# An instruction-ordering model that knows shared SBUF ports, one-piece filter loads and a new table of priorities

## The chip, the cores and the metric

The kernel runs on one core of one Trainium2 chip. The metric is the device time of one execution in microseconds; the profile has, beside it, the span from the first to the last instruction. TensorE (PE) multiplies matrices, VectorE (DVE), ScalarE (ACT) and GpSimd (POOL) work element by element, and SyncE (SP) issues all DMAs here. The engines run beside each other and wait for each other by semaphores; each runs its own instructions strictly in the order in which the program lists them.

## The reference

Two layers, each an attention and a feed-forward part, with a residual and a layer norm after each part. The input is (2, 1024, 128) in float32.

```
x = LN(x + L0_attn(x))   # 8 heads, 16 wide keys, softmax over 1024; heads summed after a reshape
x = LN(x + L0_ffn(x))    # silu(x@w1)*(x@w2), two 512x512 layers with gelu, back to 128
x = LN(x + L1_attn(x))   # 4 heads: causal convolutions, a delta rule in chunks of 32
                         # (inverse of a 32x32 triangular matrix per chunk, then a scan over chunks),
                         # a short filter (3 taps) and a long one (31 taps) on the values, gates
x = LN(x + L1_ffn(x))    # weights of +-1: 256 -> 512 -> 512 -> 128 with relu
```

## The kernel before

The rows are cut into four groups of 512, called 00, 01, 10 and 11 (batch and half). Attention of layer 0 goes in eight units (two per group): `pass1` computes the scores for the row maxima (matmuls at L814, maxima by VectorE at L816), `pass2` computes them again transposed, takes the exponential on ScalarE (L856) and multiplies with the values (L861, four 32-column matmuls at a time). `ffn0` is the feed-forward part of layer 0 (matmuls at L894, each in split precision with a high part `ahi` and a low part `alo`), `l1_attn` the delta-rule attention, and `ffn1` the last part (L1370, L1371). A group's four parts follow each other; in layer 1 a half also needs the half before it of the same batch (state of the scan, edges of convolutions and filters).

Inside `l1_attn` the stages have labels: `l1prep` and `l1gate` (projections; convolutions at L1049), `l1gram`, `l1inv` (15 steps of a product at L1144 and a sum at L1145 on VectorE, then transposes at L1155), `l1v`, `l1fir` (short filter on the vector engines, long filter as 128 small matmuls, L1210, with matrices `toep` loaded in eight pieces of 128 KB by SP, L1206, into two buffers that take turns, `nm` and `pr`), `l1T` and `l1wu` (groups of four 32x32 matmuls, one per head, L996), `l1scan` (16 dependent steps: a matmul and an addition on VectorE, L1322), `l1out`, and `l1rms` (L1354 to L1362). Layer norms take statistics on VectorE (L699, L701), the root on GpSimd (L703, L704) and the normalisation on one of them (L706).

The program is first written down part after part, and then the whole of it is put in order by a planner. `Plan.graph` builds the dependences, `Op.price` gives every instruction a duration, `Plan.run` plays the program through in time: whenever an engine is free it takes, of the instructions whose inputs are there, the one with the best rank. The rank is the time to the end along the longest chain (after `TURNS` passes back and forth), less a bonus for the part and group that the instruction belongs to, from the table `AHEAD` (in thousands of nanoseconds). The order in which the model took the instructions becomes the order on each engine, by dependences that need no waiting (`order`).

Four more numbers are in `RUN`. `switch` is what TensorE must gain in rank before it changes between full 128x128 matmuls and tiled small ones. `target` is the sum of columns that it should have streamed in the last 3.4 us of the model's time; below it, a dense matmul is taken first, and where nothing is ready, a filler matmul on the identity is put in (`dummies`; L1516 for a full one, L996 with the tile `ip` for a group of four small ones). With `rewarm` off this stops while the model holds the clock to be low.

In the model VectorE and GpSimd are independent of each other: an instruction takes its price, whatever the other engine does.

Of the kernel before, what the change touches and what calls it, by code (L numbers as in the profile page):

```python
# [14 lines left out]
AX = mybir.AxisListType  # L15

MARK = HOOK = None
RUN = {'dummies': True, 'target': 4530, 'rewarm': False, 'switch': 7026}
TURNS = 5
AHEAD = {  # L20
    "ffn0": {"00": 22.2, "01": 18.7, "10": 2.9, "11": -654.8},
    "ffn1": {"00": -153.5, "01": -136.6, "10": -65.1, "11": 9.8},
    "l1T": {"00": 30.9, "01": -81.4, "10": 95.8, "11": -6.2},
    "l1fir": {"00": -18.8, "01": -105.5, "10": -8.4, "11": 28.7},
    "l1gate": {"00": 182.7, "01": -69.9, "10": 117.6, "11": 47.2},
    "l1gram": {"00": -32.0, "01": -18.3, "10": 34.2, "11": 45.9},
    "l1inv": {"00": 41.3, "01": -12.8, "10": 61.1, "11": -56.0},
    "l1out": {"00": -63.2, "01": 33.9, "10": -9.7, "11": -10.5},
    "l1prep": {"00": 20.1, "01": 18.8, "10": 57.7, "11": 43.0},
    "l1rms": {"00": 20.0, "01": 21.9, "10": 36.6, "11": -17.4},  # L30
    "l1scan": {"00": 19.3, "01": 27.2, "10": 70.9, "11": 82.5},
    "l1v": {"00": -69.1, "01": 37.5, "10": 176.4, "11": 55.1},
    "l1wu": {"00": -18.4, "01": 13.4, "10": 15.7, "11": -37.6},
    "norm_in": {"0": 108.6, "1": -14.8},
    "pass1": {"0": 5.1, "1": -21.2, "2": -75.6, "3": -562.6, "4": 17.7, "5": 65.3, "6": 18.4, "7": 4.4},
    "pass2": {"0": -83.4, "1": -75.7, "2": -184.7, "3": 31.0, "4": 13.6, "5": 203.8, "6": 15.6, "7": 28.5},
    "post": {"00": -35.5, "01": 102.2, "10": 132.9, "11": 164.2},
    "prep": {"": 106.5},
    "stacks": {"00": 29.8, "01": 8.9, "10": 191.8, "11": -5.2},
    "stk": {"0": 105.8, "1": 140.3, "2": -27.7, "3": 95.0, "4": -83.8, "5": 45.2, "6": 57.1, "7": 134.2},  # L40
    "weights": {"": 217.5},
}
HALVES, RU = 1, 1
LEND = (4, 2)
# [35 lines left out]
class Op:  # L80


    def __init__(self, ins, n):
        self.ins, self.n = ins, n
        self.preds, self.succ = {}, []
        self.table = None
        self.cols = self.occ = self.dur = self.data = self.load = 0
        self.mode, self.dense, self.parts = None, False, [ins]
        self.e = "-"
        if ins is None:  # L90
            return
        self.e = str(ins.engine).split(".")[1]
        ap = lambda a: getattr(a, "bass_ap", None)
        self.src = [ap(a) for a in ins.ins if ap(a) is not None]
        self.dst = [ap(a) for a in ins.outs if ap(a) is not None]
        self.price()

    def price(self):
        i, kind = self.ins, type(self.ins).__name__
# [12 lines left out]
        e = self.e  # L112
# [25 lines left out]
        if e == "Activation":  # L138
            t = (51 if psum(self.src[0]) else 93) + N / 1.2 + 93 * ptr
            f = str(getattr(i, "func", "")).split(".")[-1]  # L140
            self.table = {"Gelu": 1, "Exp": 0}.get(f)
        elif e == "DVE":
            t = {"InstBNStats": 69, "InstReciprocal": 150}.get(kind, 68) + N / (0.57 if kind == "InstStreamTranspose" else 0.96) + 61 * ptr
            sb = not any(map(psum, self.src + self.dst))
            if sb and kind in ("InstTensorScalarPtr", "InstTensorCopy", "InstMemset") and sum(size(a) > 1 for a in self.src) < 2:
                t -= N / 1.92
        else:
            op = str(getattr(i, "op", ""))
            if kind == "InstMemset":
                t = 36 + N / 1.2  # L150
            elif kind == "InstTensorCopy":
                t = 120 + (0.9 if N > 200 else 3.33) * N
            elif kind == "InstTensorTensor":
                t = 150 + (180 * N if "pow" in op else 2.1 * N)
            else:
                t = 765 if ptr == 2 and N == 128 else 175 + 0.97 * N + 75 * ptr
# [3 lines left out]
class Plan:  # L160
# [205 lines left out]
    def run(self, rank, switch=0, dummies=False, target=0, rewarm=False, least=-1):  # L366
# [6 lines left out]
        ready = {e: {} for e in list(LAT) + ["-"]}  # L373
        pend, times = [], [0.0]
        free, cnt, order = dict.fromkeys(ready, 0.0), {}, {e: [] for e in ready}
        table, idle, gone_at, queue = 0, 0, None, 0
        mode, end = None, 0.0
        recent, busy = [], 0
        todo = sum(o.e == "PE" for o in ops)

        def count(t, o, cols):
# [15 lines left out]
        while len(done) < len(ops):  # L397
# [4 lines left out]
            for e, qs in ready.items():  # L402
                while free[e] <= t:
# [24 lines left out]
                                continue  # L428
                    if not best:
                        break  # L430
                    o = heapq.heappop(qs[min(best)[2]])[2]
                    occ, dur, nxt = o.occ, o.dur, t + o.occ
                    if e == "PE":
                        todo -= 1
# [30 lines left out]
def body(ctx: ExitStack, tc: tile.TileContext, A, out, dbg=None):  # L465
# [536 lines left out]
    def l1_attn(L, gi, late):  # L1002
# [178 lines left out]
        def fir():  # L1181
# [21 lines left out]
            for d in range(32):  # L1203
                if d % 4 == 0:
                    toep = own(("nm", "pr")[d // 4 % 2], (128, 2, 4, 32))
                    nc.sync.dma_start(out=toep, in_=A["toep"][:, :, d:d + 4, :].rearrange("g p d c -> p g d c"))  # L1206
                for h in range(4):
                    g, e = divmod(h, 2)
                    s = slice(64 * e, 64 * e + 64)
# [318 lines left out]
def layout(inputs):  # L1528
# [66 lines left out]
    for t in range(32):  # L1595
        w = pad[:, 31 - t:95 - t].reshape(2, 2, 32, 2, 32)
        for j in range(2):
            tp[:, :, 1 - j, t] = w[:, :, :, j]
    d["toep"] = tp.reshape(2, 128, 32, 32)
    k0 = f["L1_ffn_k0"].view(np.uint8).reshape(2, 128, 512)  # L1600
    k1 = f["L1_ffn_k1"].view(np.uint8).reshape(4, 128, 4, 128).transpose(2, 1, 0, 3).reshape(4, 128, 512)
    k2 = f["L1_ffn_k2"].view(np.uint8).reshape(4, 128, 128).transpose(1, 0, 2).reshape(1, 128, 512)
# [16 lines left out]
```

## Time and profile before

| | |
|---|---|
| runs shown | 639.54 us median of 3 (631.74, 639.54, 640.3) |
| profiled execution | 634.86 us, span 633.1 us |
| mean granted TensorE clock | 0.956 |
| instructions | 18276 |
| busy: PE, weight loads, DVE, ACT, POOL | 564.3, 366.4, 435.2, 335.0, 254.6 us |
| chain that ended last | PE 47%, DVE 14%, issue 4%, ACT 4%, DMA 2%, POOL 2% |

How to read it: shares over the whole span hide that the kernel has stages. Up to some 380 us attention and `ffn0` of the first groups run together, and afterwards `l1_attn` and `ffn1` of all four groups are left, with many small dependent instructions. A view of the trace by stretches gives busy time and granted clock for each. "issue" in the chain is time in which an engine waited for nothing that the profile shows. The matmuls' ends are modelled, so a busy PE is not one at its peak.

### The profile page before, as it was taken

The page shows a single profiled execution, that of the slowest core. Times are in us where ns is not written, and L with a number is a line of the kernel's source. Part 1 is how long each engine was busy: PE and PEld are TensorE (multiplying, and loading weights), DVE is VectorE, ACT ScalarE, POOL GpSimd, SP SyncE. Part 2 cuts the span into 40 slices and gives each one's busy share as a digit, 9 for nine tenths or more (in the row PEclk, how much of TensorE's full clock was granted, in tenths as well). Part 3 has the DMA queues.
Part 4 walks back from the last instruction along what each step waited for, and adds up shares of the span by engine and source line. Part 5 has one row for each costly group of instructions (what it writes and reads, how often), then busy time and mean ns, then how long its engine had stood idle before and what let it go on. Part 6 is the DMA issues. An engine that isn't in the chain of part 4 may idle for free.

```text
span 633.1 us, 18276 instructions
## 1 busy us (share of the span) xinstructions
PE 564.3 (89%) x7767; PEld 366.4 (58%) x7767; DVE 435.2 (69%) x1002; ACT 335.0 (53%) x599; POOL 254.6 (40%) x347
## 2 busy tenths in 40 slices
PE   2879999999999999999999998789878987689984
PEld 1245355567565565465545675566656675567773
DVE  5869777774748956748694279953879787256773
ACT  3676467755858657958778662422644220024331
POOL 9783020230403323404445972364716547124310
PEclk9999999999999999999999999989999598578998
DMA  8786220225122233131023330544202112201220
GB/s 281 256 278 235 51 50 2 47 83 145 59 68 81 37 113 104 34 107 63 1 67 103 118 119 18 183 120 149 73 5 85 37 54 71 64 27 64 77 97 17
DMA packets 30691, 57.63 MB, mean 91 GB/s; under 512 B 4049, under 2 KB 16977, under 8 KB 30610
## 3 DMA queue, kind: packets, MB, share of 16 engines
q1 hardware_dynamic: 30610, 56.47, 29.1%
q8 instruction: 61, 1.00, 0.6%
q14 instruction: 20, 0.16, 0.1%
HBM read 40.40 MB, written 8.39 MB: 77 GB/s over the span
## 4 chain that ended last, share of the span: by engine, by line
PE 47%; DVE 14%; issue 4%; ACT 4%; DMA 2%; POOL 2%; POOLq 0%; SPq 0%; DVEq 0%; ACTq 0%
PE ps L894 12%; PE ps L996 6%; PE s L854 5%; PE pv L861 5%; PE ps L814 3%; PE ps L1370 3%; PE ps L1371 3%; PE ps L1210 2%; DMA nm<-toep 2%; DVE cv L1049 2%; DVE nm L1145 1%; DVE pr L1144 1%; PE ps L1036 1%; PE ps L712 1%; DVE mp L816 1%
## 5 line engine op out<-in xcount | busy, mean ns | idle before, releaser
L816 DVE TENSOR_REDUCE mp<-ps 128x1 f32<-128x512 f32 x224 | 141.1, 683 | 56.9 <-PE ps L814 56.5
L856 ACT ACTIVATE p<-s 128x512 f32<-128x512 f32 x236 | 130.9, 601 | 42.6 <-PE s L854 34.5
L894 PE MATMUL ps<-ahi,w 128*128 128x512 f32 x352 | 119.9, 411 | 1.6 <-DVE u L926 0.9
L814 PE MATMUL ps<-k,q 128*128 128x512 f32 x240 | 87.7, 423 | 4.2 <-DVE m L822 1.6
L854 PE MATMUL s<-q,k 128*128 128x512 f32 x236 | 89.7, 420 | 0.2
L894 PEld LDWEIGHTS ps<-ahi,w 128*128 128x128 f32 x352 | 63.7, 189 | 23.5 <-issue 2.7
L861 PE MATMUL pv<-p,va 128*32 128x512 f32 x512 | 73.3, 603 | 0.0
L894 PE MATMUL ps<-alo,w 128*128 128x512 f32 x176 | 71.0, 406 | 1.9 <-POOL alo L909 1.8
L814 PEld LDWEIGHTS ps<-k,q 128*128 128x128 f32 x240 | 43.9, 188 | 35.8 <-DVE mp L816 16.4
L854 PEld LDWEIGHTS s<-q,k 128*128 128x128 f32 x236 | 42.2, 188 | 32.5 <-ACT p L856 19.6
L1370 PE MATMUL ps<-ahi,w 128*128 128x512 f32 x96 | 41.6, 434 | 2.5 <-DVE alo L1386 2.5
L931 POOL TENSOR_TENSOR alo<-u,ahi 128x512 fp32r<-128x512 f32 x16 | 20.6, 1284 | 54.2 <-ACT ahi L930 54.2
L1371 PE MATMUL ps<-alo,w 128*128 128x512 f32 x96 | 41.4, 431 | 0.1
L894 PEld LDWEIGHTS ps<-alo,w 128*128 128x128 f32 x176 | 33.3, 189 | 12.1 <-POOL alo L909 3.5
L1385 ACT ACTIVATE ahi<-ps 128x512 fp32r<-128x512 f32 x32 | 18.7, 597 | 36.3 <-PE ps L1371 36.1
L1049 DVE SCALAR_TENSOR_TENSOR cv<-pj,cvh,cv 128x512 f32<-128x512 f32 x36 | 30.5, 848 | 8.7 <-ACT cv L1045 8.2
L789 POOL MEMSET q<- 2x1024 f32 x5 | 4.7, 948 | 65.7 <-PE s L854 37.0
L703 POOL TENSOR_SCALAR r<-mv 128x4 f32<-128x4 f32 (+1 forms) x24 | 5.6, 236 | 58.7 <-DVE mv L701 58.1
L1386 DVE SCALAR_TENSOR_TENSOR alo<-ps,ahi 128x512 fp32r<-128x512 f32 x32 | 21.6, 685 | 10.9 <-ACT ahi L1385 10.7
L861 PEld LDWEIGHTS pv<-p,va 128*32 128x32 f32 x512 | 12.3, 108 | 26.3 <-issue 23.5
L909 POOL TENSOR_TENSOR alo<-z,ahi 128x512 fp32r<-128x512 f32 x8 | 10.8, 1352 | 37.7 <-PE s L854 22.9
L951 ACT ACTIVATE z<-ps,small 128x512 f32<-128x512 f32 x16 | 11.1, 691 | 27.0 <-PE ps L894 27.0
(270 smaller groups left out, 1094.1 us busy)
## 6 DMA issues: line engine op xcount, KB each, us to landing
w<-wd SPq DMA_DIRECT2D x56, 512.0 KB, 3.3
wd<-w SPq DMA_DIRECT2D x14, 512.0 KB, 3.7
raw<-wf SPq DMA_DIRECT2D x11, 256.0 KB, 3.5
pr<-toep SPq DMA_DIRECT2D x16, 128.0 KB, 3.5
nm<-toep SPq DMA_DIRECT2D x16, 128.0 KB, 2.4
pj<-vC SPq DMA_DIRECT2D x32, 64.0 KB, 2.9
q<-hi SPq DMA_DIRECT2D x14, 128.0 KB, 2.3
k<-hi SPq DMA_DIRECT2D x28, 64.0 KB, 2.4
```

The source lines that it names most:

```text
L814: nc.tensor.matmul(p, q[:, s * 128:(s + 1) * 128], d, start=True, stop=True)
L816: nc.vector.tensor_reduce(mp[:, s, e, i:i + 1], p, AX.X, ALU.max)
L854: nc.tensor.matmul(s2, ks[e][:, t * 128:(t + 1) * 128], q[:, i * 512:(i + 1) * 512], start=True, stop=True)
L856: nc.scalar.activation(p, s2, AF.Exp, scale=0.25)
L861: together([nc.tensor.matmul(pv[32 * j:32 * j + 32, :], va[:, t - 1, 2 * pr + j % 2, :], pend[j % len(pend)], start=(t == 1), stop=(t == 8 ...
L894: nc.tensor.matmul(p, w(k), a(k), start=(k == 0 and n == 0), stop=(k == nk - 1 and n == 2))
L931: nc.gpsimd.tensor_tensor(lo[:, m, :], u, hi[:, m, :].bitcast(F32), ALU.subtract)
L996: r.append(nc.tensor.matmul(p(hs), lhsT(hs), rhs(hs), start=True, stop=True, tile_position=(32 * h, 32 * h)))
L1049: nc.vector.scalar_tensor_tensor(a, pj[:, t:t + 512], cvh[:, 4 * w + t:4 * w + t + 1], a, ALU.mult, ALU.add)
L1370: nc.tensor.matmul(p, w(k), ahi(k), start=(k == 0), stop=False)
L1371: nc.tensor.matmul(p, w(k), alo(k), start=False, stop=(k == nk - 1))
L1386: nc.vector.scalar_tensor_tensor(lo, p, 0.0, hi.bitcast(F32), ALU.max, ALU.subtract)
```

## The change

Four things are edited.

1. `Op.price` notes for every instruction of VectorE and GpSimd a `lock`: on VectorE 2 for single-input copies, scalings and memsets between SBUF operands (which the model also prices at the faster rate), 1 for an instruction with more than one full SBUF operand, 0 for the rest, so for most that read PSUM; on GpSimd 1 for a memset and 2 for everything else.
2. `Plan.run` keeps for both engines until when the running instruction holds its lock. An instruction is passed over (up to four in the queue are looked at) while its lock and the other engine's running one sum to more than 2; VectorE also passes over one that would collide with the first in GpSimd's queue, if GpSimd is free and that one has the better rank. The chip's own behaviour is not touched: only the order that comes out.
3. The long filter's matrices are laid out in DRAM by piece and partition, so that a piece is one run of 1 KB in every partition instead of two of 512 B. Size and number of the loads stay.
4. `AHEAD` has new values, and in `RUN` `target` goes from 4530 to 4807 and `switch` from 7026 to 16788.

```diff
-RUN = {'dummies': True, 'target': 4530, 'rewarm': False, 'switch': 7026}
+RUN = {'dummies': True, 'target': 4807, 'rewarm': False, 'switch': 16788}
 AHEAD = {
-    "ffn0": {"00": 22.2, "01": 18.7, "10": 2.9, "11": -654.8},
-    "ffn1": {"00": -153.5, "01": -136.6, "10": -65.1, "11": 9.8},
...
+    "ffn0": {"00": 33.9, "01": 22.9, "10": -7.8, "11": -635.9},
+    "ffn1": {"00": -37.8, "01": -23.3, "10": -43.4, "11": -117.9},
...
             if sb and kind in ("InstTensorScalarPtr", "InstTensorCopy", "InstMemset") and sum(size(a) > 1 for a in self.src) < 2:
                 t -= N / 1.92
+                self.lock = 2
+            else:
+                self.lock = int(sum(size(a) > 1 and not psum(a) for a in self.src) > 1)
         else:
+            self.lock = 1 if kind == "InstMemset" else 2
...
+        hold = {"DVE": (0.0, 0), "Pool": (0.0, 0)}
...
-                    o = heapq.heappop(qs[min(best)[2]])[2]
+                    if e in hold:
+                        other = "Pool" if e == "DVE" else "DVE"
+                        until, level = hold[other]
+                        q, aside = qs[None], []
+                        rival = ready["Pool"].get(None) if e == "DVE" and free["Pool"] <= t else None
+                        o = None
+                        while q and len(aside) < 4:
+                            c = heapq.heappop(q)
+                            aside.append(c)
+                            k = c[2].lock
+                            if until > t and k and level + k > 2:
+                                continue
+                            if k and rival and rival[0][0] < c[0] and rival[0][2].lock + k > 2 and until <= t:
+                                continue
+                            o = aside.pop()[2]
+                            break
+                        for c in aside:
+                            heapq.heappush(q, c)
+                        if o is None:
+                            if until > t:
+                                heapq.heappush(times, until)
+                            break
+                        if o.lock:
+                            hold[e] = t + o.occ, o.lock
+                    else:
+                        o = heapq.heappop(qs[min(best)[2]])[2]
...
-                    nc.sync.dma_start(out=toep, in_=A["toep"][:, :, d:d + 4, :].rearrange("g p d c -> p g d c"))
+                    nc.sync.dma_start(out=toep, in_=A["toep"][d // 4])
...
-    d["toep"] = tp.reshape(2, 128, 32, 32)
+    d["toep"] = tp.reshape(2, 128, 8, 4, 32).transpose(2, 1, 0, 3, 4).copy()
```

## The prediction

> **What bounds the kernel now.** I read the stretches by engine first, then the granted clock in the late stretch, then the chain of waits and the contention between VectorE (DVE) and GpSimd (POOL). Stretch by stretch (columns: stretch, busy us and instructions of PE, PEld, DVE, ACT, POOL, then granted clock, DMA share, GB/s):
>
> ```profile
> 27.00:110.00 83.00, 78.40 (x349) 39.75 (x352) 65.53 (x139) 53.73 (x104) 28.14 (x37) 1.00 0.44 133
> 110.00:235.00 125.00, 122.62 (x605) 75.82 (x598) 88.09 (x164) 83.18 (x144) 32.71 (x35) 1.00 0.28 79
> 235.00:310.00 75.00, 73.83 (x418) 44.07 (x416) 50.59 (x99) 55.57 (x95) 24.41 (x37) 1.00 0.22 68
> 310.00:380.00 70.00, 68.54 (x1008) 42.54 (x1011) 40.63 (x93) 52.85 (x91) 45.05 (x63) 1.00 0.29 93
> 380.00:440.00 60.00, 49.05 (x1171) 35.36 (x1163) 41.40 (x109) 17.52 (x27) 25.06 (x28) 0.97 0.37 115
> 440.00:470.00 30.00, 25.20 (x817) 17.59 (x816) 23.82 (x60) 15.58 (x31) 16.12 (x28) 1.00 0.17 56
> 470.00:530.00 60.00, 52.26 (x1496) 39.22 (x1496) 52.27 (x148) 18.13 (x39) 32.67 (x46) 0.89 0.19 55
> 530.00:577.00 47.00, 35.67 (x1565) 30.27 (x1554) 20.68 (x50) 8.73 (x20) 15.01 (x16) 0.64 0.16 45
> ```
>
> The reader is to see three kernels in one. From 27 to 380 us TensorE is busy 343.4 of 353 us: no order of the other engines brings more than the 9.6 us that are left. From 440 to 530 VectorE is busy 76.1 of 90 us and sets the pace. From 530 to 577 nobody is full: VectorE works 20.7 of 47 us, and the clock is 0.64. Cut at the steps of the clock:
>
> ```profile
> 491.60:505.20 13.60, 13.32 (x247) 9.82 (x247) 9.48 (x24) 2.18 (x4) 7.95 (x14) 0.50 0.19 43
> 505.20:532.50 27.30, 22.45 (x901) 17.62 (x900) 24.77 (x79) 6.75 (x15) 15.05 (x16) 1.00 0.21 61
> 532.50:563.20 30.70, 22.78 (x1001) 19.84 (x1005) 10.28 (x34) 2.36 (x4) 7.43 (x9) 0.50 0.20 56
> ```
>
> 44.3 us lie at half clock, where, in the second of them above all, PE has small 32- and 64-row matmuls and few dense ones. The chain there is PE and "issue"; the list of waits (us, times, longest) says how much the small matmuls waited for nothing visible:
>
> ```profile
> PEld ps L996 <- issue: 24.0, 39, 2.2
> ```
>
> Now the contention that the new model knows. VectorE's timeline, then GpSimd's, around one convolution:
>
> ```profile
> 444.39 3.44 DVE L1049 SCALAR_TENSOR_TENSOR cv<-pj,cvh,cv 128x512 f32<-128x512 f32 x3
> ...
> 446.02 1.26 POOL L909 TENSOR_TENSOR alo<-u,ahi 128x512 fp32r<-128x512 f32 x1
> ```
>
> Three such steps should take 3 x 0.752 (the median of L1049) = 2.26 us; they took 3.44, because the last started at 446.04, beside GpSimd's subtraction, and lasted 1.80. Taking every group's excess over its usual length, VectorE lost some 20 us and GpSimd 13 over the span, 8 of VectorE's between 400 and 550. In the head the same is seen:
>
> ```profile
> 11.48 4.70 DVE L706 TENSOR_SCALAR xt<-xt,mv,r 128x128 f32<-128x128 f32 x8
> 12.42 2.09 POOL L563 TENSOR_SCALAR k<-small 128x1024 fp32r<-128x1024 f32 x2
> ```
>
> **The change part by part.** The matmuls and vector instructions stay: the built programs hold the same ones, in another order. New are 71 filler matmul groups (136 for 65; of them 57 full ones of two passes, 0.11 us each, and 14 of four small matmuls). Four of 17 activation-table loads go (13 are left). So nearly everything is order, and I take it by stage.
>
> *Head.* Two loads of raw weights (0.87 us of issue) leave the front of SP's queue, so x, wtmp and small start 0.9 us sooner. GpSimd no longer does 2.48 us of weight subtractions and 1.6 us of small scales ahead of the row statistics; VectorE's reduction of wv (1.22 us, after a wait of 1.07) now stands behind the eight normalisations. By rows: statistics ready 0.9 sooner, 0.24 + 0.15 + 0.95 + 1.05 us on GpSimd to the first r, so the first normalisation starts near 9.2 instead of 11.48; the second r comes 1.3 later, and the last normalisation ends near 12.2 instead of 16.18. Gain 4.0 at most 5.5, at least 0 (if the matrices ws and wg, moved behind the normalisations, come late). On SP's queue the two weight loads now stand behind wv and three loads of x; what they feed is first read by ffn0:00, at 119 us, so nothing waits there. Behind the head TensorE is full, so the gain lasts.
>
> *27 to 380.* Same matmuls, the same 116 changes between attention's dense and 32-column matmuls; by order the feed-forward of group 10 ends at the same place in PE's sequence. I take 0, from +6 (a worse interleaving of the exponentials, L856, whose waits on PE are 34.5 us in all) to -6 of the 9.6. Four table loads of 1.28 us fall away late in this stretch, three of the old ones on the chain at 344 to 350 us: 5.1 at most, 0 at least, 2 taken, since ACT is only 53 of 70 us busy there.
>
> *Long filter's matrices.* 32 loads of 128 KB in pieces of 1 KB instead of 512 B:
>
> ```profile
> DMA to landing us min/median/max: 2.2/3.3/4.6
> ```
>
> The chain holds three of these landings (406.4, 429.9 and 433.8 us), 12.5 us in all. A load of 256 KB in 2 KB pieces (raw<-wf) lands in 3.5, so packets cost something: with half of them between 0 and 6.2 us (half the 12.5) fall away; a loss is excluded, since bytes are equal and packets fewer. I take 2. The Trainium skill speaks against this part: "DMA: Bandwidth & Descriptors", Specifications, puts line rate at 512 B and more, which by itself would make this term 0 and the sum 2 us smaller.
>
> *440 to the end of group 10's scan (529.8).* VectorE's instructions priced with their own durations in this execution: 426.2 us stand ahead of and in that scan's last step before, 420.0 after. The inversion of group 11 (12.5 us) and its value path move behind; the normalisation after group 01 and all of ffn1:00 move ahead. That is -6.2; of the 5 or so us of contention in this stretch I expect less than half, -1.8. Together -8; bounds -11 and +3 (PE in order: group 10's T and wu matmuls, 80 groups, now stand in one block, and a scan step waits behind it).
>
> *From there to group 11's scan (577.7).* The 26 us in which VectorE idled now take the moved inversion. But the inversion is a chain, followed by values, filter, T, wu; and PE gets 29 more matmuls of ffn1:01 here (0.23 us, 6.7) and some 20 full fillers (0.22, 4.4). Against it, dense work between the filter's matmuls keeps the clock up: at half clock a dense pass took 0.43 instead of 0.23 and 128 small ones 2.38 against 1.87 (the rate at 459 us), some 8 us over 532 to 563, and the issue waits get cover, some 2. Net +1, bounds -8 and +12.
>
> *Tail.* Group 11's last scan steps (0.95 us each near 590, 0.8 before) no longer share VectorE with ffn1:01's last normalisation: -2, bounds -3 and +6 (26 full fillers behind the last scan step, 5.7 us, if they meet ready work; 12 before).
>
> Sum: -4 + 0 - 2 - 2 - 8 + 1 - 2 = -17. The profiled execution took 634.86 (span 633.1): 617.9. The median of the runs shown, 639.54, is 1.0074 times that execution, so the forecast in its terms is 622.4, 2.7% less. Its own range, with the terms not all failing together, is 612 to 627.
>
> **The rivals.** *Little survives.* The timetable is fitted to a model; on the chip small waits shift everything, collisions come back elsewhere, and only head and filter remain, -6: 628.9, in the median's terms 633.5. For it: the late stage's 1 to 2 us issue waits, which no priority orders. Against: 6.2 us of VectorE work really stand behind the scan.
>
> *The clock falls in the new blocks.* After the change T, wu and out of group 11, 96 groups of small matmuls, follow each other with 3 small fillers between, and before them T and wu of group 10 likewise; that is what went with 0.50 above. If half clock holds from group 10's T to group 11's scan's end, 74 dense passes cost 0.20 more (15 us), 38 fillers of two passes 0.105 more each (8), some 1,250 small matmuls 4 ns more (5): 28 us, and the VectorE and tail gains do not come, as PE sets the pace. -8 + 28 = +20: 654.9, that is 659.7, slower. It passes 2% from +13, when three quarters of that stretch lie at half. Against it: twice the fillers, and ffn1:01 now beside both filters.
>
> *The clock stays whole.* Both low stretches vanish: of 44.3 us half, less the 8 counted, -13 more: 604.9, that is 609.
>
> **How the numbers follow.** Forecast 0.48, clock whole 0.07, little survives 0.30, clock falls 0.15. The predicted time is 622.4; the range 609 to 654 leaves out about one in twenty below and most of the slow case's upper half. Faster by over 2% (about what a measurement of this kernel can tell from no change): 0.55; within 2%: 0.30; slower: 0.15.
>
> **What would show it.** Head: the last xt normalisation ends near 12 us, TensorE's first projection (L606) starts near 13. Contention: L1049's mean falls from 848 towards 752 ns. Filter: landing median under 3.3. VectorE stretch: group 10's scan ends near 514. Clock: the stretch around ffn1:01 shows 1.00, the one of T and wu of group 11 perhaps 0.50. The tail from group 11's last scan step stays near 40 us. I am wrong if the scan of group 10 does not end 10 us sooner, or if the 48 us behind it become 60.

## The result, and the profile after

The changed kernel takes 640.39 us (median of 20 runs, 635.61 to 645.59) beside 636.62 of the kernel before: ratio 1.0086, 95% interval 1.006 to 1.0112. It is slower by 0.9%, inside 2%. Forecast was 2.7% less time. Ratios here leave out the runs more than 1.5% above the fastest of their kernel, so they need not be the quotient of the medians beside them, which are of all runs (that quotient is 1.0059 here). Its profiled execution took 641.19 us, span 639.4 (before 634.86 and 633.1). The two traces differ by 6.3 us, somewhat more than the medians (3.8), and can be compared stage by stage.

The stretches of the prediction in the trace after (columns as there: stretch, busy us and instructions of PE, PEld, DVE, ACT, POOL, then clock, DMA share, GB/s):

```profile
380.00:440.00 60.00, 51.71 (x1127) 36.90 (x1127) 35.51 (x86) 18.95 (x30) 31.61 (x38) 0.91 0.39 122
440.00:470.00 30.00, 26.63 (x865) 19.80 (x865) 23.68 (x68) 15.95 (x32) 10.63 (x19) 1.00 0.17 55
470.00:530.00 60.00, 48.34 (x1713) 40.79 (x1711) 39.84 (x141) 13.41 (x30) 27.91 (x43) 0.91 0.15 43
530.00:577.00 47.00, 36.28 (x1133) 30.30 (x1135) 27.12 (x62) 10.05 (x18) 18.35 (x21) 0.86 0.30 88
```

Look at 470 to 530: VectorE, busy for 52.27 of these 60 us before, is busy for 39.84 now. The stretch is no longer VectorE's. The next stretch has VectorE at 27.12 instead of 20.68 and its clock at 0.86 instead of 0.64, and still the whole takes longer.

On contention, the convolution's line among the costliest groups (busy us, mean ns of one):

```profile
L1080 DVE SCALAR_TENSOR_TENSOR cv<-pj,cvh,cv 128x512 f32<-128x512 f32 x36 | 28.1, 786 | 3.4 <-ACT cv L1076 3.0
```

On the small matmuls, the list of waits (us, times, longest):

```profile
PEld ps L1027 <- issue: 27.9, 40, 2.2
```

On the filter's matrices, the view of their tile:

```profile
DMA to landing us min/median/max: 2.2/2.3/3.9
```

The convolution step fell from 848 to 786 ns. Summed over all groups, as in the prediction, VectorE's excess over the usual lengths (an estimate of what collisions cost it) fell from 20.4 to 6.8 us, and behind 400 us from 9.2 to 0.1. So most of the collisions that the lock is to avoid are gone. The small matmuls' issue waits (24.0 before) did not shrink, and the filter's loads land sooner.

Where the 6.3 us come from, by the end of each stage's last VectorE step (each trace's instructions put beside the program's order):

| up to | before | after | this stage | forecast |
|---|---|---|---|---|
| `stk` 0 (head) | 29.4 | 25.4 | -4.0 | -4 |
| `l1scan` 00 | 399.8 | 387.9 | -7.9 | 0, table loads -2, part of the filter's -2 |
| `l1rms` 00 | 440.1 | 429.8 | +1.6 | rest of the filter's |
| `l1scan` 10 | 529.8 | 523.6 | +4.1 | -8 |
| `l1scan` 11, start | 577.7 | 584.2 | +12.7 | +1 |
| end of the span | 633.1 | 639.4 | -0.2 | -2 |

The changed kernel leads by 11.9 us at group 00's scan. By the start of group 11's scan it is 6.5 us behind.

### The profile page after: what moved, and what is told of

Read it like the earlier page. It is cut to its first block, busy times and chain, and to the rows that moved or that the text cites. A ratio compares the mean times of both kernels' runs of the same rounds, so it can differ in the third digit from the quotient of the medians.

```text
span 639.4 us, 18702 instructions
## 1 busy us (share of the span) xinstructions
PE 577.2 (90%) x7993; PEld 384.6 (60%) x7993; DVE 418.1 (65%) x1002; ACT 329.3 (52%) x595; POOL 251.6 (39%) x347
## 4 chain that ended last, share of the span: by engine, by line
PE 74%; issue 6%; DVE 6%; DMA 5%; POOL 4%; ACT 3%; SPq 2%; POOLq 0%; DVEq 0%; ACTq 0%
PE ps L925 19%; PE pv L892 10%; PE s L885 10%; PE ps L845 9%; PE ps L1027 8%; DMA nm<-toep 4%; PE ps L1067 2%; PE ps L1401 2%; PE ps L1402 2%; PE ps L1241 2%; PE ps L743 1%; PE ip L1547 1%; PE ip L1027 1%; DMA raw<-wf 1%; PE ps L1317 1%
## 5 line engine op out<-in xcount | busy, mean ns | idle before, releaser
L925 PE MATMUL ps<-ahi,w 128*128 128x512 f32 x352 | 123.1, 418 | 0.4 <-ACT u L978 0.4
L885 PE MATMUL s<-q,k 128*128 128x512 f32 x236 | 92.5, 428 | 0.2 <-ACT p L887 0.2
L845 PE MATMUL ps<-k,q 128*128 128x512 f32 x240 | 85.1, 417 | 3.1 <-DVE m L853 1.6
L925 PEld LDWEIGHTS ps<-ahi,w 128*128 128x128 f32 x352 | 65.5, 192 | 22.6 <-ACT p L887 2.5
L925 PE MATMUL ps<-alo,w 128*128 128x512 f32 x176 | 71.1, 408 | 0.3 <-POOL alo L940 0.3
L1401 PE MATMUL ps<-ahi,w 128*128 128x512 f32 x96 | 40.5, 422 | 1.0 <-DVE alo L1417 1.0
L1402 PE MATMUL ps<-alo,w 128*128 128x512 f32 x96 | 39.7, 413 | 0.8 <-DVE alo L1411 0.5
L1080 DVE SCALAR_TENSOR_TENSOR cv<-pj,cvh,cv 128x512 f32<-128x512 f32 x36 | 28.1, 786 | 3.4 <-ACT cv L1076 3.0
L1547 PE MATMUL ip<-mats 128*128 128x128 f32 x186 | 30.0, 297 | 0.0
L1547 PEld LDWEIGHTS ip<-mats 128*128 128x128 f32 x186 | 27.0, 208 | 1.2
```

The costliest lines, as they stand in the source:

```text
L845: nc.tensor.matmul(p, q[:, s * 128:(s + 1) * 128], d, start=True, stop=True)
L885: nc.tensor.matmul(s2, ks[e][:, t * 128:(t + 1) * 128], q[:, i * 512:(i + 1) * 512], start=True, stop=True)
L925: nc.tensor.matmul(p, w(k), a(k), start=(k == 0 and n == 0), stop=(k == nk - 1 and n == 2))
L1080: nc.vector.scalar_tensor_tensor(a, pj[:, t:t + 512], cvh[:, 4 * w + t:4 * w + t + 1], a, ALU.mult, ALU.add)
L1401: nc.tensor.matmul(p, w(k), ahi(k), start=(k == 0), stop=False)
L1402: nc.tensor.matmul(p, w(k), alo(k), start=False, stop=(k == nk - 1))
```

## Experiments

All ratios are to the kernel before, run on the same chip beside it. Lines of kernels with more code are shifted: L1027, L1241 and L1353 of the changed kernel are L996, L1210 and L1322 before, and L1052, L1266 and L1378 in the hybrid.

### Halves and parts of the change

One piece per partition alone, in the order before:

```diff
-                    nc.sync.dma_start(out=toep, in_=A["toep"][:, :, d:d + 4, :].rearrange("g p d c -> p g d c"))
+                    nc.sync.dma_start(out=toep, in_=A["toep"][d // 4])
```

> The kernel before with one thing changed: the long filter's matrices lie in one 1 KB run per partition; the order on every engine stays that of before. Theory A (packets cost time; three landings of 12.5 us were on the chain before, and the median landing fell from 3.3 to 2.3 us in the changed kernel): 2 to 4 us faster than before, ratio 0.994 to 0.997, landing median near 2.3. Theory B (the landings are waited for only where TensorE would wait anyway): 0.999 to 1.001 with the same landing median.

Measured: 639.17 us, 1.0023 (0.9988 to 1.0059). The landings, in this kernel's view of the tile:

```profile
DMA to landing us min/median/max: 2.0/3.2/3.8
```

The median is 3.2, where it was 3.3 before; so the 2.3 of the changed kernel comes from when its loads run, not from their pieces. There is no gain to measure.

The changed kernel without its 136 fillers:

```diff
     order = plan.order["PE"]
+    order[:] = [o for o in order if not isinstance(o, tuple)]
+    plan.idle = 0
```

> The changed kernel in its own order, without its 136 groups of filler matmuls (before has 65). Theory A (fillers stand on the path: 12 us of the chain of the changed kernel are fillers, against 5 before): 6 to 12 us faster than the changed kernel, 628 to 634. Theory B (the fillers pay for themselves by the clock): more than 90 us at half clock instead of 51, and 5 to 15 us slower than the changed kernel, 645 to 655. Theory C (they fill waits that are there anyway, and the clock does not matter for what sets the pace): within 2 us of the changed kernel.

Measured: 637.36 us, 1.0009 (0.998 to 1.0038). Half clock rises from 56.8 to 114.1 us in all, and the time does not rise: the ratio with them was 1.0086. None of the three theories gave this range. In this order the fillers cost somewhat more time than the clock that they keep gives back.

That is a net figure, and it does not make half clock free. Every run has its span and mean granted clock on record, and the traces show full and half clock alone, so each run's time at half can be estimated. In 88 runs of the kernel before it goes from 47 to 91 us, and each microsecond more goes with 0.27 us more time; in the 20 runs of the changed kernel with 0.31, in the 12 without fillers with 0.21. Which is cause and which effect no run shows. If it is the clock, the 53 us more of it without fillers (105 against 52 in the mean of the runs) cost some 11 to 16 us, and leaving out the fillers paid that back.

Two hybrids. Both plans are made, the new one with the lock, the old one without; every instruction that the old plan starts no later than the last step of `l1scan` 00 is taken in the one order, the rest in the other. Both have the one-piece filter:

```diff
+CUT, LATE = "l1scan:00", "old"             # "new" in the second
...
+    old, when = planned(AHEAD_OLD, RUN_OLD, False)
+    new, _ = planned(AHEAD, RUN, True)
+    cut = max(when[o] for o in old["DVE"] if label(o) == CUT)
+    first = {o for o in when if when[o] <= cut}
...
+    head, tail = (new, old) if LATE == "old" else (old, new)
+    plan.order = {e: part(head[e], True) + part(tail[e], False) for e in new}
```

> New order up to the set of instructions that the old plan had started by the end of group 00's scan (some 400 us in the profile of before), old order for all that follows, and the new filter loads. Theory A (the new order gains some 10 us up to there, as group 00's scan ends at 388 instead of 400, and the loss is in the late order alone): 624 to 629 against 636.6 of before, faster by 1.2 to 2%. Theory B (the lead is only apparent, since work was left for later): within 3 us of before.

> The mirror image: old order up to that set, new order for the rest, new filter loads. Theory A (the late order is what costs): 645 to 654, slower than before by 1.4 to 2.7%, and slower than the changed kernel. Theory B (the late order is as good as the old one, and something in the first part costs): within 3 us of before or faster.

Measured: new, then old, 628.46 us, 0.9835 (0.9796 to 0.9874; the medians of all runs give 0.9856); old, then new, 651.07 us, 1.0228 (1.0187 to 1.0269). Both are what theory A expected, and the two add up (-1.65% and +2.28% give +0.6%, measured +0.86%). This settles which half does what: the new order is worth 10 us up to group 00's scan and costs 14 behind it. The first hybrid beats both kernels, the one before by 1.65% (1.4% by the medians). Its convolution step among the costliest groups:

```profile
L1105 DVE SCALAR_TENSOR_TENSOR cv<-pj,cvh,cv 128x512 f32<-128x512 f32 x36 | 30.5, 848 | 3.8 <-ACT cv L1101 3.3
```

848 ns, as before the change: of the two, the faster kernel has more of VectorE's excess, 14.9 us against 6.8. Collisions are not what decides behind 440 us.

The lock with the old table (`AHEAD` and `RUN` as before), and the new table with the lock off (`if False:` for `if e in hold:`), both with the one-piece filter:

> The kernel before with the lock in the planner and the filter in one piece, but the old table. Here group 11's Gram stands behind the whole scan of group 10. Theory A (the place of group 11's inverse sets the end): the Gram starts only near 515 us, and the time is 645 or more, over the changed kernel's. Theory B (the lock itself saves VectorE about 14 us of collisions and only the new table gives them back): 625 to 632.

> The new table and the filter in one piece, but the planner doesn't know the lock. Here group 11's Gram stands in the middle of group 10's scan steps, and its filter and T directly behind group 10's filter, as in the kernel before. Theory A (place of group 11's inverse): near the kernel before, 634 to 642, with VectorE's collisions back near 20 us. Theory B (the new table itself costs, whatever the planner knows): 645 or more.

Measured: 683.7 us, 1.0707 (1.0657 to 1.0757), and 665.28 us, 1.042 (1.0373 to 1.0467). Both are far slower than either whole. With the lock alone group 11's convolutions start at 522.6 us (469.0 in the changed kernel) and its Gram ends at 545.6. The table alone is 9.5 us behind the kernel before at `pass1` 0 and 14 at `l1rms` 00; its time is what theory B named. A table is fitted to its planner; "lock" and "table" have no gains of their own that could be summed. VectorE's excess is 9.8 and 12.9 us in them, so the lock saves collisions under either table (12.9 to 6.8 under the new one, 20.4 to 9.8 under the old), and no time under the old one.

### Is it group 11's late inverse?

What struck in the trace after: VectorE waits in a stretch that it had filled. Its row from 480 to 524 us (columns as above), of the kernel before, the faster hybrid and the changed kernel:

```profile
480.00:524.00 44.00, 38.27 (x1130) 30.34 (x1133) 37.40 (x107) 13.44 (x30) 25.20 (x38) 0.84 0.21 61
480.00:524.00 44.00, 36.66 (x1339) 28.11 (x1331) 37.60 (x105) 8.65 (x20) 26.03 (x39) 0.88 0.19 49
480.00:524.00 44.00, 35.50 (x1396) 29.45 (x1395) 27.64 (x97) 5.58 (x12) 23.33 (x37) 0.88 0.10 28
```

VectorE is busy for 27.64 of 44 us in the changed kernel; before it was 37.40, and in the faster hybrid it is 37.60. Its longest waits in that stretch (us in total, times, longest), first of the kernel before:

```profile
DVE tt L1246 <- PE ps L996: 2.5, 1, 2.5
DVE tt L1322 <- PE ps L996: 1.3, 1, 1.3
```

Then of the changed kernel:

```profile
DVE oC L1377 <- PE ps L1027: 5.5, 1, 5.5
DVE kv L1304 <- PE ps L1027: 4.0, 2, 2.8
DVE rs L1385 <- ACT sq L1383: 3.8, 1, 3.8
```

And of the hybrid, new order first, then old:

```profile
DVE tt L1378 <- PE ps L1052: 2.5, 4, 1.6
DVE tt L1302 <- PE ps L1052: 2.4, 1, 2.4
```

Before and in the hybrid, group 11's inverse (11 to 13 us of short VectorE steps) fills the gaps of group 01's scan steps. After, the scan of 01 is through at 492.8 and the inverse starts at 511.8, since the last three of 16 Gram groups stand among group 10's wu on TensorE; in between VectorE waits for out (`oC`), wu (`kv`) and ScalarE's squares (`rs`). It is done at 541.1 instead of 527.6. Theory A says that this late inverse is the loss. Two numbers of the table test it:

```diff
-    "l1gram": {"00": -6.9, "01": -32.9, "10": 193.6, "11": -55.0},
+    "l1gram": {"00": -6.9, "01": -32.9, "10": 193.6, "11": 45.9},
```

> The changed kernel with one number of the table altered, so that the Gram matrices of group 11 go ahead of group 10's wu and group 01's out on TensorE; all else is in the changed order up to there. Theory A (what the changed kernel loses is group 11's inverse, which starts 16 us late, and the chain v, copies, filter, T, wu behind it): the Gram ends near 500 us instead of 512, the inverse near 531 instead of 541, the scan of group 11 near 592 instead of 600, and the time is about 632, 1.2% under the changed kernel's. Theory B (the inverse isn't the bound; half clock and issue waits in the chain of small blocks behind it are): the Gram moves and the scan of group 11 still ends within 3 us of 600; time 638 to 642.

and with 95.9 there and 60 instead of -0.1 for `l1inv` 11:

> As the experiment with group 11's Gram first, and its inverse ahead on every engine too. Theory A (late inverse): the inverse ends near 526 to 530 us, the scan of group 11 near 588, time 628 to 632. Theory B (the chain behind the inverse is the bound at any place): 638 to 642. Theory C (VectorE has no room there, so a sooner inverse only delays the scan of group 10): the scan of group 10 ends 5 us or more after 523.6, and the time stays within 3 us of the changed kernel's 640.

Measured: 652.91 us, 1.0238 (1.019 to 1.0286), and 640.15 us, 1.0038 (1.0002 to 1.0073). The Gram ends at 496.1 and 493.2, but the inverse at 538.5 and 535.7: VectorE takes it up and then holds it behind steps that wait for wu and scan of group 10. Group 11's scan ends at 600.2 and 599.3, as in the changed kernel (600.0). The first is slower for another reason, late in the tail: its out of group 11 now alternates with ffn1 of group 10, and `l1rms` 11 ends at 626.5 instead of 614.8. In the second theory B's signs came (scan within 3 us of 600, time 638 to 642), and no gain over the changed kernel is shown. Theory A earned nothing here, but was not yet given its inverse.

Next the finished order itself was edited by hand, nothing planned anew: each engine's order is sorted by planned start, the keys of some steps are changed, and what they read is drawn along (or, moved later, what reads them is pushed).

```diff
+    for o in chosen:                       # l1gram, l1inv, l1v of group 11; by = -12 us
+        key[o] += by
...
+    for o in reversed(line):
+        key[o] = min([key[o]] + [key[s] for s, _ in o.succ])
```

The second kernel moves the inverse alone, by -15 us; the third moves Gram, inverse and v of the hybrid's late order by +12 us, T and wu of group 11 staying in blocks.

> The changed kernel's own order, with one thing moved by hand: group 11's Gram matrices, inverse and v stand 12 us sooner in the planned order on every engine (with what they read); nothing is planned anew, the same 136 fillers, filter, T, wu and scan of group 11 keep their places. Theory A (VectorE idles in 480 to 524 us because group 11's inverse isn't there to fill the waits of the scan steps, and the inverse is then on the chain behind): VectorE's waits of 16 us in that stretch fall to 10 or less, the inverse ends by 530 instead of 541, and the time is 628 to 634. Theory B (in this order VectorE can't be filled, the scan steps in front of TensorE set the pace): the inverse moves, the scan of group 10 ends 5 us or more later than 523.6 and the time stays at 637 or more.

> The changed kernel's own order, with group 11's inverse alone 15 us sooner, which draws the last Gram groups before wu of group 10; v of group 11 stays late. Theory A: the inverse ends near 528, but v ends only near 540, so that a part is left: 632 to 638. Theory B (scan steps set the pace): 637 or more, with the scan of group 10 later.

> The mirror of it: the hybrid (new order up to group 00's scan, old order behind) with group 11's Gram, inverse and v 12 us later in the order, and what hangs on them no sooner than they. Theory A: VectorE's waits in 480 to 524 rise from 6 us by 6 to 10, the inverse ends 10 us later than 519.9, and the time is 634 to 641 instead of 628.5. Theory B (the place of the inverse isn't what costs): 626 to 631.

Measured: 664.44 us, 1.0444 (1.0391 to 1.0498); 652.13 us, 1.028 (1.0227 to 1.0333); and in the hybrid 642.11 us, 1.0144 (1.0095 to 1.0194). The first is inconclusive: drawing group 11's convolutions along held up group 10's inverse (506.9 instead of 487.4), and its own inverse was no sooner (546.8). In the second the inverse ended 11 us sooner (530.2), v 10 us later (553.9) and the scan of group 10 10.5 us later (534.1): theory B's signs. The third is a hit for theory A: 12 us later in the good late order cost 14 us by the times and 3.1% by the ratios, and VectorE's busy time in 480 to 524 fell from 37.60 to 26.34. But v moved along, and the filters behind it were drawn out (41.6 us instead of 30.7, in the table below). So in the old order the place of inverse and v matters; whether it is what the new one lacks had to be tried with the gap itself.

```diff
+    at3 = key[row[2]]                      # third step of l1inv 11, on top of the last table
+    for n, o in enumerate(row[3:] + v):    # v = steps of l1v 11, in the second kernel only
+        key[o] = min(key[o], at3 + 0.01 * n)
```

> The changed kernel with group 11's Gram and inverse first (1.0038), and the 36 steps of that inverse in one row behind its third step on VectorE, GpSimd and ScalarE, ahead of group 10's wu and scan steps; TensorE's order stays. Theory A (VectorE's gap can be filled and the late inverse is the loss): the inverse ends near 515 us instead of 536, group 10's scan stays within 3 us of 522, v of group 11 still ends near 540, so the time falls by 0 to 4 us, to 636 to 640. Theory C (no room): group 10's scan ends 6 us or more later, time 645 or more.

> The same with v of group 11 directly behind the inverse. Theory A: v ends near 520 us, its copies and the filter of group 11 follow 15 us sooner, and the time is 628 to 634. Theory B (TensorE's queue: filter, T and wu of group 11 stand behind ffn1 of group 01): v is sooner, wu of group 11 starts within 4 us of 569, and the time stays at 636 to 641. Theory C (no room on VectorE): group 10's scan ends 6 us or more later than 522, time 645 or more.

Measured: 644.12 us, 1.0082 (1.0044 to 1.012; g1 below), and 648.52 us, 1.0179 (1.0118 to 1.0239; g2). The last two steps of the inverse in VectorE's timeline (start, us), first of the changed kernel:

```profile
538.53 1.04 DVE L1186 STREAM_TRANSPOSE tt<-xn 128x512 f32<-128x512 f32 x1
540.02 1.04 DVE L1186 STREAM_TRANSPOSE nB<-xn 128x512 f32<-128x512 f32 x1
```

Then with the inverse in the gap:

```profile
506.66 1.04 DVE L1186 STREAM_TRANSPOSE tt<-xn 128x512 f32<-128x512 f32 x1
507.55 1.01 DVE L1186 STREAM_TRANSPOSE nB<-xn 128x512 f32<-128x512 f32 x1
```

32 us sooner, with group 10's scan only 2.6 us later (526.2), and nothing of it reaches the end: the ratio is that of the changed kernel, where theory A had 636 to 640 us. So the gap has room for the inverse, and filling it gains nothing. For v as well there was no free room: in g2 group 10's scan ends at 530.7, 7.1 us later than in the changed kernel, and with the time over 645 both signs of theory C came. Theory A has fallen as the sole cause.

### What else holds group 11's chain

Two things stand ahead of T and wu of group 11 in the new order that did not before. One is `ffn1` of group 01: 56 of its groups of matmuls stand ahead of wu's first on TensorE, 8 before. The other is the filter. Its matrices come in eight pieces per group, in two buffers, so that a piece's load waits until the matmuls two pieces earlier are done. First and last matmuls of both groups' filters in TensorE's timeline (start, us), before:

```profile
529.43 0.78 PE L1210 MATMUL ps<-pj,nm 64*32 64x16 f32 x32
...
560.10 0.63 PE L1210 MATMUL ps<-pj,pr 64*32 64x16 f32 x32
```

And after, with two of the rounds:

```profile
523.15 0.69 PE L1241 MATMUL ps<-pj,nm 64*32 64x16 f32 x31
...
553.60 0.45 PE L1241 MATMUL ps<-pj,nm 64*32 64x16 f32 x32 [1.09 <-DMA nm<-toep]
553.93 0.45 PE L1241 MATMUL ps<-pj,pr 64*32 64x16 f32 x32
557.82 0.45 PE L1241 MATMUL ps<-pj,nm 64*32 64x16 f32 x32 [0.49 <-DMA nm<-toep]
...
563.90 0.31 PE L1241 MATMUL ps<-pj,pr 64*32 64x16 f32 x13 [2.54 <-issue]
```

Before, the two groups' pieces alternate in SyncE's queue and one group's loads run beside the other's rounds: 31.3 us from first to last. After, group 11's eight come behind group 10's, in rounds of two every 4 us: 41.1 us. Its chain of waits has them (start, us):

```profile
547.27 2.01 DMA pj<-vC
549.79 3.76 DMA nm<-toep
554.12 3.66 DMA nm<-toep
```

Four kernels took these apart, all with Gram and inverse first and the gap filled unless said otherwise. g3: the filter of group 11 and its T and wu moved up in TensorE's queue. j1: all but one of those groups moved under the scan steps of group 11, four behind each; j2: the same in the changed order with all but ten, inverse late. k1: v behind group 10's fifth scan step on VectorE, and the pieces of the two filters in turn in SyncE's and TensorE's queues.

```diff
+    for n, o in enumerate([o for o in pe("ffn1:01") if key[o] >= low]):    # j1, j2
+        key[o] = steps[min(15, n // 4)] + 0.01
...
+    for n, o in enumerate(loads11):                                        # k1; pe11 likewise
+        key[o] = min(key[o], key[inv[-1]] + 0.01 * (n + 1) if n < 2 else key[loads10[n // 2 * 2 + 1]] + 0.01)
```

> The same as the run before, and on TensorE group 11's filter and T stand ahead of most of group 01's ffn1, its wu behind two thirds of it. Theory B: wu of group 11 starts 8 us or more sooner than 569, its scan ends near 588 instead of 599, and the time is 626 to 632. If the chain is bound by something else (copies into the column layout, landings of the filter's matrices, half clock), wu starts within 4 us of 569 and the time is 636 or more.

> As g2 (group 11's Gram, inverse and v early, 1.0179), and on TensorE all but one of ffn1's matmuls of group 01 that stood ahead of group 11's T and wu now stand between the scan steps of group 11, four behind each; their VectorE and ScalarE steps move along. Theory Q (TensorE's queue holds group 11's chain): its wu starts near 560 us instead of 576, the scan ends near 592 instead of 607 and the time is 630 to 640. Theory R (the chain is bound by its own steps, or the scan of group 11 grows by what is put under it): the scan ends within 4 us of 607, time 645 or more.

> The changed kernel's order with only that move: ffn1's matmuls of group 01 behind group 11's wu, the inverse and v late as they are (541 and 544 us). Theory Q with two bounds in a row: the inverse, v, copies and filter then hold T, which starts near 562 instead of 568; wu starts 3 to 7 us sooner than 570 and the time is 633 to 638. If the queue alone is the bound: wu starts 10 us or more sooner, 626 to 632. Theory R: 638 or more.

> As g1 (group 11's Gram first and its inverse in VectorE's gap, 1.0082, wu of group 11 from 572.6 us, scan to 603.1), with v of group 11 behind the fourth scan step of group 10, and the loads and matmuls of group 11's filter in turn with those of group 10's in SyncE's and TensorE's queues, as in the order before; ffn1 of group 01 keeps its place. Theory S (two filters in series set when T and wu of group 11 start): the filters' matmuls span about 31 to 34 us instead of 39, wu of group 11 starts 5 to 9 us sooner than in g1, and the time is 633 to 639, 0.985 to 1.0 of before. Theory R (the chain is bound elsewhere): the filters end sooner, wu stays within 3 us of 572.6 and the time at 641 or more.

Measured, with the earlier kernels beside them (us; ends and starts by VectorE's steps of the stage; the filters' first to last matmul, in brackets its length):

| kernel | inverse ends | v ends | scan 10 ends | filters | wu 11 starts | scan 11 | ratio |
|---|---|---|---|---|---|---|---|
| before | 527.6 | 525.8 | 529.8 | 529.4 to 560.7 (31.3) | 564.4 | 577.7 to 592.5 | 1 |
| hybrid, new then old | 519.9 | 518.1 | 522.1 | 521.7 to 552.4 (30.7) | 556.4 | 569.8 to 584.6 | 0.9835 |
| hybrid, Gram, inverse, v later | 533.7 | 530.9 | 520.4 | 519.6 to 561.2 (41.6) | 569.5 | 584.7 to 599.8 | 1.0144 |
| changed | 541.1 | 544.0 | 523.6 | 523.1 to 564.2 (41.1) | 570.3 | 584.2 to 600.0 | 1.0086 |
| g1, inverse | 508.6 | 543.7 | 526.2 | 525.8 to 564.8 (39.0) | 572.6 | 584.6 to 603.1 | 1.0082 |
| g2, inverse and v | 508.9 | 513.8 | 530.7 | 530.4 to 569.2 (38.8) | 576.5 | 589.3 to 607.4 | 1.0179 |
| g3, queue | 507.2 | 512.2 | 530.6 | 528.7 to 564.0 (35.3) | 577.8 | 596.6 to 618.0 | 1.0322 (1.0252 to 1.0392) |
| j1, `ffn1` under the scan | 508.8 | 513.8 | 530.6 | 530.2 to 566.1 (35.9) | 574.6 | 589.9 to 633.8 | 1.0631 (1.054 to 1.0722) |
| j2, the same alone | 535.9 | 537.9 | 525.6 | 525.0 to 563.0 (38.0) | 571.3 | 585.5 to 622.2 | 1.0364 (1.029 to 1.0439) |
| k1, filters in turn | 509.0 | 522.6 | 531.8 | 531.5 to 555.0 (23.5) | 580.2 | 591.5 to 608.3 | 1.026 (1.0216 to 1.0303) |

First set the end of group 10's scan against the start of wu. Between them lie 34.6 and 34.3 us in the first two rows, the old late order as it was planned, and 44.0 to 49.1 in the other eight, wherever the inverse stands (46.7 in the changed kernel, 46.4 in g1). Of the 12.7 us that the changed kernel loses up to group 11's scan, 12.1 lie there. The theories by which a relieved queue brings wu sooner (B in g3, Q in j1 and j2, S in k1) all failed: wu starts 1.0 to 9.9 us later than in the changed kernel in each of the last six rows.

Now read the columns from left to right. In g2 v is 30 us sooner, and the filters do not start sooner: they start where group 10's scan ends, and group 11's stand behind group 10's in the queues. In g2, g3, j1 and k1 that scan ends 7.0 to 8.2 us later than in the changed kernel; g2 differs from g1, where it is 2.6, only in v. In j1 `ffn1` is out of the way, the filters end at 566.1 and hold T and wu, whose place on TensorE is behind the last of them. In k1 the filters end at 555.0, 9 us sooner than in the changed kernel, and wu starts later still. VectorE's waits in k1 from 524 to 600 us say for what:

```profile
DVE alo L1417 <- ACT ahi L1416: 14.3, 7, 6.1
DVE alo L1411 <- ACT ahi L1410: 11.0, 2, 10.3
```

22 of these 25 us are behind steps of `ffn1` of group 01, with T of group 11 queued behind them. So inverse, filter and `ffn1` each stand ahead of T and wu. That whichever one is taken away uncovers the next within some microseconds is the likeliest reading; it is not shown apart from what each edit cost by itself. The runs show no single seat of the 14 us; only the old late order, which has all three out of the way, brings wu to 556.4. A kernel with the changed late order and all three relieved at once, group 10's scan left in its place, was not built. g3 and the j kernels also paid for their own edits (g3 put group 10's last pieces behind group 11's T, j1 and j2 stretched a scan of 16 us to 44 and 37), so that their ratios are no measure of their idea.

### Fillers in the faster order

The first hybrid without its 64 fillers:

> The hybrid without its 64 filler matmuls. If fillers in this order cost TensorE more than the clock that they keep, as the changed kernel without its 136 suggests (ratio to before 1.0009 against 1.0086), the time is 622 to 627, with about 30 us more of half clock. If the clock is worth more, 630 or over.

Measured: 627.74 us, 0.9891 (0.9844 to 0.9938), beside 0.9835 (0.9796 to 0.9874) with them in another set of runs. The intervals overlap: no difference shown. Only for the 136 of the changed order is a cost shown.

## Why the prediction was wrong

It was wrong in direction, and two steps of it carry the whole error. The forecast was -17, the measured difference of the traces +6.3, a miss of 23.3 us. Both of its own signs of being wrong came: the scan of group 10 ended 6.2 us sooner and not 10, and the 48 us behind it became 60.6.

*440 to group 10's scan: -8 forecast, +4.1 measured.* Here the step failed, not its size. The instructions ahead of that scan's last step were counted by duration on VectorE, as if VectorE went on being full. That holds only while it has something to do at every moment. The order took away just the short steps of group 11's inverse that had filled its waits; what stayed waits for TensorE. The prediction did name the mechanism ("a scan step waits behind it", T and wu of group 10 in one block) and gave it +3 at most; measured it is the 4.0 of `kv <- ps` and the 5.5 of `oC <- ps` above. The collisions (-1.8 forecast here) went away more thoroughly than forecast, and the stretch got longer all the same.

*From there to group 11's scan: +1 forecast, +12.7 measured, bound +12.* The step that failed is the path behind the inversion, which the sum had at next to nothing: 12.1 of the 12.7 us are a longer way from group 10's scan to wu of group 11 (46.7 us instead of 34.6). The inversion was given the "26 us in which VectorE idled"; it did get them. What was missing was the queue behind it: v, eight copies, eight loads in rounds of two, T, wu, each behind group 10's or group 01's work on SyncE and TensorE. The prediction counted 29 more matmuls of `ffn1` (6.7 us) and fillers (4.4) and then paid for them with a better clock. The clock came, 0.86 instead of 0.64, and did not pay for that path. Which of the queues holds it, and for how much, stays open.

*Filter: -2 forecast, 0 measured* (1.0023, 0.9988 to 1.0059). Both prices were on the table; the row of 256 KB loads was the wrong neighbour. The Trainium skill's rule, in "DMA: Bandwidth & Descriptors", Specifications, that pieces of 512 B already move at line rate, agrees with the landing of 3.2 us in 1 KB pieces beside 3.3 in 512 B.

*Head: -4 forecast, -4.0 measured* at 25 us: the last normalisation ends at 11.53 us and the first starts at 7.51 instead of 11.48:

```profile
7.51 0.34 DVE L737 TENSOR_SCALAR xt<-xt,mv,r 128x128 f32<-128x128 f32 x1 [1.98 <-POOL r L735]
...
7.91 3.62 DVE L737 TENSOR_SCALAR xt<-xt,mv,r 128x128 f32<-128x128 f32 x7
```

"So the gain lasts" is not shown: `pass1` 0 ends at 49.3 us, 49.0 before. In between the clock is at half from 35.1 to 42.0, which it was not before, but that is not the reason: the first hybrid has the same order there and full clock until 391.8 us, and its `pass1` 0 ends at 49.7. On ScalarE the last exponential of `pass2` 0 ends at 80.0 instead of 85.6, so the lead may have gone over to other work. No run took that apart.

*27 to 380: 0 and -2 for the table loads forecast, -7.9 measured* from there to group 00's scan; the bounds were -6 and -5.1. TensorE is busy for 348.5 of the 353 us from 27 to 380, 343.4 before, and VectorE's excess before 400 us fell by 4.5. The hybrid shows that this half is real and worth 1.65%; which of its moves earn it, the table loads among them, was not tried.

*Tail: -2 forecast, -0.2 from the start of group 11's scan.*

Of the rivals, "little survives" was nearest in kind: small waits shift everything behind the model's back. "The clock falls in the new blocks" had the right sign by the wrong way: half clock sums to 56.8 us after and 58.2 before, and in the mean of all runs to 52 and 71 (the estimate above). The changed kernel lost with the better clock.

## What to carry to other kernels

Before a stretch is priced by the busy time of the engine that fills it, ask which short, free steps fill that engine's waits now, and whether the new order still has them there; if they go, the stretch is priced by the waits. A chain moved later is priced by every queue that it joins, and if several queues end within a few microseconds of each other, an experiment that relieves one may show nothing; cut the kernel into halves in time and swap those, as the hybrids did. A planner's table and its model are fitted together: each half of such a change alone was 4% and 7% slower than what it came from, so a hand-made order that is slower says little against its idea.

## What had not been expected of the hardware

The hybrid, with 14.9 us of VectorE's excess, has a span of 625.2 us; the changed kernel, with 6.8, has 639.4. Fewer collisions did not mean less time here, though no run changed the collisions alone. And a microsecond at half clock went with about 0.3 us of time in the runs of both kernels, less than the half that would be lost if TensorE were busy throughout. The 136 fillers that kept the clock cost as much as that or more: the ratio is 1.0086 with them and 1.0009 without, at 57 us more of half clock in the traces.
